# Silu on ScalarE in place of the tanh form, and the first layer's sums moved from VectorE to ScalarE

## The chip, the cores and the metric

The kernel runs on one core of one Trainium2 chip. Its metric is the device time of one execution in microseconds. The engines are named as in the profile: PE is TensorE (PEld its weight loads), DVE is VectorE, ACT is ScalarE, POOL is GpSimd, SP is SyncE, which issues nearly all of the DMAs. Every engine works through its own list of instructions in order; semaphores hold an instruction back until what it reads is there.

## What is computed

The input is x, 16 batches of 512 tokens with 256 features, all float32. Four layers follow one another, each on the normalized x and added to x:

```python
x = x + mamba(layernorm(x), ...)        # selective scan: h = exp(dt*A)*h + inp, 16 states per feature
x = x + ffn(layernorm(x), ...)          # the same FFN weights twice
x = x + linear_attention(layernorm(x), ...)   # 16 heads of 16, causal
x = x + ffn(layernorm(x), ...)
```

The FFN quantizes its input, its weights and its hidden values to 4-bit floats in blocks of 16 along the last dimension, and computes

```python
gate = fp4_linear(x, w_gate)            # 256 -> 704
y    = fp4_linear(x, w_up)              # 256 -> 704
h    = silu(gate) * y                   # silu(g) = g * sigmoid(g) = 0.5 * g * (1 + tanh(g/2))
return fp4_linear(h, w_down)            # 704 -> 256
```

## The kernel before

A batch goes through four stages: `scan` (mamba and, woven into it, the prologue of the next batch), the first FFN (`ffn` with the letter "f"), `attention`, and the second FFN (`last_ffn`, letter "g"). Each stage is a Python generator; what it yields is the cost in microseconds of VectorE that it puts on its last piece. `run_all` (L866) keeps several stages under way and always draws from the one that is least far on, its progress being the yielded cost over the constant of its kind (`SCAN, FFN, ATTN`, L863). So at one time the scan of batch b, the first FFN of batch b-1, the attention of batch b-2 and the second FFN of batch b-3 are written into the engines' lists piece by piece. The constants and the yields thus decide how the stages lie among one another. After the weights' preparation and the first scans the program repeats itself from batch to batch; below, one such repeat is called a period.

In `scan`, each batch takes 16 steps (L533 to L575). A step needs a tile `bar` of two rows of 512: it is fetched by a DMA from DRAM (L520), ACT raises it to exponentials (Exp at L527, twice, then Square at L530), DVE scans over it (L548) and multiplies (L552), and PE sums it over the states (L558). There are four `bar` buffers, so a fetch is issued when the scan of four steps earlier has ended, and ACT has it next in its list after the other work that was written ahead of it.

`front` (L435) is the first part of the prologue. It takes the mean and variance of the coming batch's x for the first layer's normalization: `bn_stats` (L442) and `bn_aggr` (L443) on DVE for each of the four chunks of 128 tokens, then `inverse` (L389), a small DVE instruction and a power on POOL that give 1/sqrt(var + eps). `to_features` (L412) turns x into features by rows with diagonal matrices that ACT makes of the result (L424). For the other layers the sums come from elsewhere: DVE adds up the row sums while it adds the residual (`residual`, L373), and ACT adds up the squared distances from the mean (`distances`, L382 to L386, an activation Square with bias and an accumulated sum).

`ffn` (L583) normalizes, quantizes (`fp4_steps`, L225), transposes, and then goes over four chunks of 128 tokens. `hidden` (L596) computes one chunk's 704 hidden values in two halves of 352. Per half, PE fills two PSUM banks, `pg` with the gate and `pu` with the up projection (L605, two matmuls each over the contraction); ACT computes tanh(gate/2) (L611); DVE computes (1 + tanh) * gate (L612) and then 0.5 * that * up (L613). Then `fp4` quantizes the hidden chunk: five DVE passes over 704 elements, with one on ACT between them (L248, the tile `big`). `down` (L619) transposes it on PE, ACT copies it out of PSUM (L631, L636, tile `hqT`), and PE multiplies by the down weights (L640); DVE adds the result to x (L377 or L647). There are seven PSUM banks for all that passes through `bank`.

ACT's functions come in table sets, and an instruction that loads a table stands in its list wherever the next function is in another set than the last. Before, ACT uses Exp, Tanh, Ln, Abs, Relu, Square and copies. Its list holds 33 table loads: 16 ahead of the Ln at L472, 16 ahead of the next Tanh (L611) or Exp (L527) that follows it, and one at the start.

Of the kernel before, what the change touches and what calls it, by code (L numbers as in the profile page):

```python
# [32 lines left out]
def kernel(  # L33
# [45 lines left out]
    def bank(name):  # L79
        return ps.tile([P, 512], F32, tag="bank", name=name)  # L80
# [287 lines left out]
    def summed(i, name):  # L368

        sums = small.tile([P, NC], F32, tag=f"sum{i}", name=f"sum_{name}")  # L370
        dist = small.tile([P, NC], F32, tag=f"dist{i}", name=f"dist_{name}")
        return sums, dist
# [16 lines left out]
    def inverse(i, var, by, name):  # L389

        shifted = small.tile([P, NC], F32, tag=f"var{i}", name=f"var_{name}")
        nc.vector.tensor_scalar(shifted, var, by, LN_EPS, ALU.mult, ALU.add)
        rstd = small.tile([P, NC], F32, tag=f"rstd{i}", name=f"rstd_{name}")
        nc.gpsimd.tensor_tensor(rstd, shifted, neg_half, ALU.pow)
        return rstd
# [38 lines left out]

    def front(b, xt):  # L435

        stats = small.tile(
            [P, NC, nc.vector.BN_STATS_DIM], F32, tag="stats", name=f"st_m{b}"
        )
        mv = small.tile([P, NC, nc.vector.BN_AGGR_DIM], F32, tag="mv", name=f"mv_m{b}")  # L440
        for c in range(NC):
            nc.vector.bn_stats(stats[:, c, :], xt[:, c, :])  # L442
            nc.vector.bn_aggr(mv[:, c, :], stats[:, c, :])  # L443
        rstd = inverse(2, mv[:, :, 1], 1.0, f"m{b}")
        yield 2.4
        turned[b] = to_features(one, xt, f"m{b}", rstd)
        yield 1

# [134 lines left out]
    def ffn(i, nm, b, xs):  # L583
        xt = xs[b]
        act = acts[i]
        xq = layernorm(i, xt, stats.pop((nm, b)), f"{nm}{b}")
        if i == 0:
            stats["a", b] = summed(2, f"a{b}")
        key, nm = ("a", b), f"{nm}{b}"
        yield 2.2  # L590
        fp4(act, xq.rearrange("p c d -> p (c d)"), NC * D, nm)
        yield 7
        xqT = to_features(act, xq, nm)
        yield 1

        def hidden(c):  # L596

            h = act.tile([P, FF], F32, tag="h", name=f"h_{nm}_{c}", bufs=2)
            for f in range(2):
                cols = ts(f, HF)  # L600
                pg = bank(f"pg_{nm}_{c}_{f}")
                pu = bank(f"pu_{nm}_{c}_{f}")
                for pw, wT in ((pg, wgT), (pu, wuT)):
                    for k in range(ND):
                        nc.tensor.matmul(  # L605
                            pw[:, :HF], xqT[:, k, ts(c, P)], wT[:, k, cols],
                            start=(k == 0), stop=(k == ND - 1),
                        )

                hc = h[:, cols]  # L610
                nc.scalar.activation(hc, pg[:, :HF], AF.Tanh, scale=0.5)  # L611
                nc.vector.scalar_tensor_tensor(hc, hc, 1.0, pg[:, :HF], ALU.add, ALU.mult)  # L612
                nc.vector.scalar_tensor_tensor(hc, hc, 0.5, pu[:, :HF], ALU.mult, ALU.mult)  # L613
                yield 1
            fp4(act, h, FF, f"{nm}_{c}")
            hs.append(h)
            yield 5

        def down(c, h):  # L619

            hqT = act.tile([P, NR, P], F32, tag="hqT", name=f"hqT_{nm}_{c}", bufs=2)
            for r0 in range(0, NR, 4):
                r1 = min(r0 + 4, NR)
                pt = bank(f"pt_h_{nm}_{c}_{r0}")
                for r in range(r0, r1):
                    rows = min(P, FF - r * P)
                    nc.tensor.transpose(
                        pt[:rows, ts(r - r0, P)], h[:, r * P : r * P + rows], ident
                    )
                full = min(r1, NF)  # L630
                nc.scalar.copy(  # L631
                    hqT[:, r0:full, :],
                    pt[:, : (full - r0) * P].rearrange("p (r t) -> p r t", t=P),
                )
                if r1 > NF:
                    nc.scalar.copy(hqT[:TAIL, NF, :], pt[:TAIL, ts(NF - r0, P)])  # L636
            po = bank(f"po_{nm}_{c}")
            for r in range(NR):
                rows = min(P, FF - r * P)
                nc.tensor.matmul(  # L640
                    po[:, :D], hqT[:rows, r, :], wdT[:rows, r, :],
                    start=(r == 0), stop=(r == NR - 1),
                )
            if key in stats:
                residual(xt, c, po[:, :D], stats[key])
            else:
                nc.vector.tensor_tensor(xt[:, c, :], xt[:, c, :], po[:, :D], ALU.add)  # L647


        hs = []  # L650
        yield from hidden(0)
        for c in range(NC):
            if c + 1 < NC:
                yield from hidden(c + 1)
            down(c, hs[c])
            yield 0.5
# [203 lines left out]
        nc.sync.dma_start(out[b].rearrange("(c p) d -> p c d", p=P), xs[b])  # L860


    SCAN, FFN, ATTN = 65.7, 40.2, 25.7  # L863

    def run_all(stages):

# [62 lines left out]
```

## Time and profile before

| | |
|---|---|
| median of 3 runs | 2825.38 us (2824.58 to 2828.75) |
| the profiled execution's own time | 2823.49 us |
| its span, first to last instruction | 2821.8 us |
| mean granted TensorE clock | 0.942 |
| period, from one Ln load (L472) to the next | 162 to 165 us |
| first Ln load of a fully mixed period, last Ln load | 595.7 us, 2245.8 us |
| ACT busy in one period (911 to 1074 us) | 92.06 of 163 us |

The span thus has a fill of nearly 600 us, ten like periods, and a drain of nearly 580 us in which no scan is left. Busy time of an engine is the time in which one of its instructions was on record; consecutive instructions of DVE and ACT overlap by some 0.1 us in the records. "Idle before" is the time an engine stood still ahead of an instruction, with who ended it.

### The profile page before, as it was taken

What the parts mean: (1) busy time and instruction counts of PE and PEld (TensorE: products, weight loads), DVE (VectorE), ACT (ScalarE), POOL (GpSimd) and SP (SyncE); (2) the same over time, 40 slices, a digit from 0 to 9 for tenths busy, and PEclk for the clock granted to TensorE, in tenths of its full rate; (3) what the DMA queues carried; (4) which work ended last, traced back from release to release, by engine and by line L of the source; (5) the groups of instructions that cost most, each with busy time, mean ns of one, the idle gap of its engine ahead of it and who ended that gap; (6) DMA issues with size and microseconds to landing.
All of it is one profiled execution on the core that took longest, in us unless ns stands there. A gap on an engine that the chain in (4) does not pass through costs nothing.

```text
span 2821.8 us, 34272 instructions
## 1 busy us (share of the span) xinstructions
PE 2449.7 (87%) x12907; PEld 1441.9 (51%) x12907; DVE 2430.5 (86%) x3689; ACT 1492.1 (53%) x2846; POOL 172.2 (6%) x171
## 2 busy tenths in 40 slices
PE   5677989799898989989898998989899898889886
PEld 3234545455555555555555555555555554556564
DVE  7898888898999898899989889998988999868465
ACT  4776564465646455464645556464555646333321
POOL 2000000000000010000001000000100000000000
PEclk7788999899999999999999999999999999999897
DMA  5533212222223131322313132131213213000000
GB/s 142 131 93 82 64 49 53 67 53 83 52 60 76 38 75 45 82 53 54 82 38 75 45 82 53 47 89 38 75 45 83 53 45 82 24 8 1 8 8 8
DMA packets 97146, 165.01 MB, mean 58 GB/s; under 512 B 8434, under 2 KB 92372, under 8 KB 96980
## 3 DMA queue, kind: packets, MB, share of 16 engines
q1 hardware_dynamic: 95360, 161.77, 22.3%
q8 instruction: 101, 1.65, 0.3%
q10 hardware_dynamic: 1620, 1.06, 0.1%
q14 instruction: 65, 0.53, 0.1%
HBM read 146.02 MB, written 16.78 MB: 58 GB/s over the span
## 4 chain that ended last, share of the span: by engine, by line
DVE 40%; PE 36%; DMA 9%; ACT 9%; issue 3%; POOL 2%; SPq 0%; POOLq 0%; ACTq 0%; DVEq 0%
DVE h L548 15%; DMA bar<-dd 9%; PE pg_g L605 5%; DVE h L552 4%; PE pu_g L605 4%; PE po_g L640 4%; PE pg_f L605 3%; PE pu_f L605 3%; PE py L558 3%; ACT bar L527 2%; PE pz L457 2%; DVE v_f L244 2%; DVE sm L729 2%; PE pqk L678 2%; ACT bar L530 1%
## 5 line engine op out<-in xcount | busy, mean ns | idle before, releaser
L548 DVE TENSOR_TENSOR_SCAN h<-bar,inp 128x1024 f32<-128x1024 f32 x256 | 579.4, 2277 | 13.9 <-PE py L558 7.6
L527 ACT ACTIVATE bar<-bar,a_col 128x511 f32<-128x511 f32 x512 | 352.4, 715 | 339.6 <-DMA bar<-dd 291.5
L558 PE MATMUL py<-h,red 128*32 128x512 f32 x1024 | 288.7, 645 | 119.3 <-DVE h L552 118.2
L552 DVE TENSOR_TENSOR h<-h,cm 128x1024 f32<-128x1024 f32 x256 | 311.1, 1218 | 0.6
L530 ACT ACTIVATE bar<-bar 128x1022 f32<-128x1022 f32 x256 | 269.3, 1052 | 3.0
L640 PE MATMUL po_g<-wdT,hqT_g 128*128 128x256 f32 (+1 forms) x768 | 214.3, 425 | 41.8 <-ACT hqT_g L631 41.8
L640 PEld LDWEIGHTS po_g<-wdT,hqT_g 128*128 128x128 f32 (+1 forms) x768 | 149.0, 206 | 120.3 <-ACT hqT_g L631 65.1
L640 PE MATMUL po_f<-wdT,hqT_f 128*128 128x256 f32 (+1 forms) x768 | 198.2, 400 | 9.6 <-ACT hqT_f L631 9.6
L605 PE MATMUL pg_g<-wgT,tT_g 128*128 128x352 f32 x512 | 190.7, 492 | 0.3 <-DVE sm L729 0.3
L640 PEld LDWEIGHTS po_f<-wdT,hqT_f 128*128 128x128 f32 (+1 forms) x768 | 137.5, 192 | 94.6 <-ACT hqT_f L636 29.0
L605 PE MATMUL pu_g<-wuT,tT_g 128*128 128x352 f32 x512 | 182.3, 480 | 0.0
L605 PE MATMUL pg_f<-wgT,tT_f 128*128 128x352 f32 x512 | 181.8, 478 | 0.0
L605 PE MATMUL pu_f<-wuT,tT_f 128*128 128x352 f32 x512 | 172.7, 460 | 3.4 <-DVE sm L729 3.0
L729 DVE TENSOR_TENSOR sm<-psc,causal 128x512 f32<-128x512 f32 x256 | 163.9, 681 | 10.8 <-PE psc L722 5.9
L611 ACT ACTIVATE h_g<-pg_g 128x352 f32<-128x352 f32 x128 | 59.1, 462 | 195.3 <-PE pg_g L605 195.1
L558 PEld LDWEIGHTS py<-h,red 128*32 128x32 f32 x1024 | 37.8, 110 | 221.6 <-DVE h L552 171.4
L605 PEld LDWEIGHTS pu_g<-wuT,tT_g 128*128 128x128 f32 x512 | 103.3, 202 | 60.7 <-issue 11.4
L763 POOL COPY dx<-den 128x256 f32<-128x256 f32 x64 | 42.2, 660 | 1482.7 <-PE pr L768 795.5
L248 ACT ACTIVATE big_f<-v_f 128x704 bf16<-128x704 f32 (+1 forms) x80 | 67.2, 840 | 122.3 <-DVE v_f L244 122.3
L605 PEld LDWEIGHTS pg_f<-wgT,tT_f 128*128 128x128 f32 x512 | 96.3, 196 | 66.9 <-issue 23.2
L612 DVE SCALAR_TENSOR_TENSOR h_g<-h_g,pg_g 128x352 f32<-128x352 f32 x128 | 65.5, 512 | 74.2 <-ACT h_g L611 72.8
L678 PE MATMUL pqk<-tT_a,w_qkv_sb 128*128 128x512 f32 x256 | 121.6, 614 | 7.4 <-ACT tT_a L430 7.4
(237 smaller groups left out, 4707.0 us busy)
## 6 DMA issues: line engine op xcount, KB each, us to landing
bar<-dd SPq DMA_DIRECT2D x256, 511.0 KB, 4.7
x<-in_L_attn_a_x_dram SPq DMA_DIRECT2D x16, 512.0 KB, 4.5
dd<-dt SPq DMA_DIRECT2D x128, 64.0 KB, 1.7
out_dram<-x SPq DMA_DIRECT2D x16, 512.0 KB, 4.4
w_qkv_sb<-in_L_attn_b_W_attn_dram ACTq DMA_DIRECT2D x1, 768.0 KB, 7.1
raw_d<-in_L_ffn_w_down_dram SPq DMA_DIRECT2D x1, 704.0 KB
raw_g<-in_L_ffn_w_gate_dram SPq DMA_DIRECT2D x1, 640.0 KB, 7.1
raw_u<-in_L_ffn_w_up_dram SPq DMA_DIRECT2D x1, 640.0 KB, 6.5
```

The source lines that it names most:

```text
L248: nc.scalar.activation(big, v, AF.Abs, scale=STEP)
L527: nc.scalar.activation(bar[:, i, 1:S], bar[:, i, 1:S], AF.Exp, scale=a_col[:, g : g + 1])
L530: nc.scalar.activation(bar[:, :, 1:S], bar[:, :, 1:S], AF.Square)
L548: nc.vector.tensor_tensor_scan(h.rearrange("p i t -> p (i t)"), bar.rearrange("p i t -> p (i t)"), inp.rearrange("p i t -> p (i t)"), 0.0, ...
L552: nc.vector.tensor_tensor(h, h, cm.unsqueeze(1).to_broadcast([P, 2, S]), ALU.mult)
L558: nc.tensor.matmul(py[32 * q : 32 * q + 32, :], red[:, j, :], (h0, h)[q // 2][:, q % 2, :], start=False, stop=(j == 3),)
L605: nc.tensor.matmul(pw[:, :HF], xqT[:, k, ts(c, P)], wT[:, k, cols], start=(k == 0), stop=(k == ND - 1),)
L611: nc.scalar.activation(hc, pg[:, :HF], AF.Tanh, scale=0.5)
L612: nc.vector.scalar_tensor_tensor(hc, hc, 1.0, pg[:, :HF], ALU.add, ALU.mult)
L640: nc.tensor.matmul(po[:, :D], hqT[:rows, r, :], wdT[:rows, r, :], start=(r == 0), stop=(r == NR - 1),)
L678: nc.tensor.matmul(pz, w_qkv_sb[:, k, ts(je, P)], xnT[:, k, :], start=(k == 0), stop=(k == ND - 1),)
L729: nc.vector.tensor_tensor(t, psc[g].rearrange("p (s t) -> p s t", t=P), causal.unsqueeze(1).to_broadcast([P, NH // 4, P]), ALU.mult,)
```

## The change

It has three parts. In `hidden`, the gate banks of both halves are filled one behind the other, ACT computes Silu of each directly into h, and after a yield the two up banks are filled and DVE multiplies them in with one instruction per half; the DVE instruction with the gate (L612) is gone. In `front`, ACT takes the place of DVE: a Copy with an accumulated sum for each chunk, then the squared distances by the helper that the other layers use. And the constants and yields by which the stages are interleaved are lowered.

```diff
     def front(b, xt):
 
-        stats = small.tile(
-            [P, NC, nc.vector.BN_STATS_DIM], F32, tag="stats", name=f"st_m{b}"
-        )
-        mv = small.tile([P, NC, nc.vector.BN_AGGR_DIM], F32, tag="mv", name=f"mv_m{b}")
+        sums, dist = summed(0, f"m{b}")
         for c in range(NC):
-            nc.vector.bn_stats(stats[:, c, :], xt[:, c, :])
-            nc.vector.bn_aggr(mv[:, c, :], stats[:, c, :])
-        rstd = inverse(2, mv[:, :, 1], 1.0, f"m{b}")
-        yield 2.4
+            nc.scalar.activation(squares, xt[:, c, :], AF.Copy, accum_out=sums[:, c : c + 1])
+            distances(xt, c, sums, dist)
+        rstd = inverse(2, dist, 1.0 / D**3, f"m{b}")
+        yield 0.2
         turned[b] = to_features(one, xt, f"m{b}", rstd)
         yield 1
...
             h = act.tile([P, FF], F32, tag="h", name=f"h_{nm}_{c}", bufs=2)
-            for f in range(2):
-                cols = ts(f, HF)
-                pg = bank(f"pg_{nm}_{c}_{f}")
-                pu = bank(f"pu_{nm}_{c}_{f}")
-                for pw, wT in ((pg, wgT), (pu, wuT)):
+
+            for wT, what in ((wgT, "pg"), (wuT, "pu")):
+                for f in range(2):
+                    cols = ts(f, HF)
+                    pw = bank(f"{what}_{nm}_{c}_{f}")
                     for k in range(ND):
                         nc.tensor.matmul(
                             pw[:, :HF], xqT[:, k, ts(c, P)], wT[:, k, cols],
                             start=(k == 0), stop=(k == ND - 1),
                         )
-
-                hc = h[:, cols]
-                nc.scalar.activation(hc, pg[:, :HF], AF.Tanh, scale=0.5)
-                nc.vector.scalar_tensor_tensor(hc, hc, 1.0, pg[:, :HF], ALU.add, ALU.mult)
-                nc.vector.scalar_tensor_tensor(hc, hc, 0.5, pu[:, :HF], ALU.mult, ALU.mult)
-                yield 1
+                    if what == "pg":
+                        nc.scalar.activation(h[:, cols], pw[:, :HF], AF.Silu)
+                    else:
+                        nc.vector.tensor_tensor(h[:, cols], h[:, cols], pw[:, :HF], ALU.mult)
+                yield 0.5
             fp4(act, h, FF, f"{nm}_{c}")
...
-    SCAN, FFN, ATTN = 65.7, 40.2, 25.7
+    SCAN, FFN, ATTN = 63.5, 36.2, 25.7
```

In the lists of instructions that the changed program gives the engines, there are 192 table loads on ACT where there were 33: one at the start, 16 ahead of the Ln, 87 ahead of a Silu, 88 ahead of an Exp (86 of the scan's, 2 of the attention's). The numbers of PE's, POOL's and SP's instructions are the same but for the merging of rows, and their order is another where the stages are interleaved otherwise.

## The prediction

> **What bounds the kernel now.** I read the page's busy shares first: DVE and PE are both near nine tenths, ACT at half.
>
> ```profile
> PE 2449.7 (87%) x12907; PEld 1441.9 (51%) x12907; DVE 2430.5 (86%) x3689; ACT 1492.1 (53%) x2846; POOL 172.2 (6%) x171
> ...
> DVE 40%; PE 36%; DMA 9%; ACT 9%; issue 3%; POOL 2%; SPq 0%; POOLq 0%; ACTq 0%; DVEq 0%
> ```
>
> The chain that ended last passes to and fro between DVE and PE, with ACT on it for 9% of the span (about 260 us, a sixth of ACT's busy time). Then the busy times by windows, for one period:
>
> ```profile
> 911.00:950.00 39.00, 37.74 (x157) 23.70 (x158) 33.42 (x62) 22.46 (x36) 0.84 (x1) 0.96 0.15 37
> ...
> 911.00:1074.00 163.00, 147.90 (x802) 87.12 (x802) 147.92 (x227) 92.06 (x176) 10.27 (x9) 0.98 0.24 61
> ```
>
> After the length, the columns are PE, PEld, DVE and ACT busy. PE and DVE carry 148 us each of 163, so neither alone sets the period: their imbalance stretch by stretch does. In the first 39 us, the gate and up products of the FFNs, PE is full and DVE waits. Next the groups by line and the waits:
>
> ```profile
> L612 DVE SCALAR_TENSOR_TENSOR h_f<-h_f,pg_f 128x352 f32<-128x352 f32 x128 | 65.8, 515 | 68.2 <-ACT h_f L611 68.1
> L612 DVE SCALAR_TENSOR_TENSOR h_g<-h_g,pg_g 128x352 f32<-128x352 f32 x128 | 65.5, 512 | 74.2 <-ACT h_g L611 72.8
> ...
> L442 DVE BATCH_NORM_STATS2 st_m<-x 128x6 f32<-128x256 f32 x64 | 24.3, 398 | 0.1
> ```
>
> ```profile
> ACT bar L527 <- DMA bar<-dd: 291.5, 152, 6.1
> ACT h_g L611 <- PE pg_g L605: 195.1, 96, 5.8
> ```
>
> L612, which the change removes, is also where DVE waits longest (141 us). But the second fence shows where that comes from: ACT itself waits there for PE's gate product, and elsewhere it stands at the head of its list for a `bar` fetch (291 us), with all behind it held.
>
> **DVE's saving.** Records of DVE overlap: an L612 of 0.51 us at 917.79 is followed by L819 at 918.22. With overlaps counted once, the 256 L612 hold 119 us and the `bn_stats` and `bn_aggr` rows (64 each) 26 us. L613 becomes a product of the same two operands and keeps its 507 ns (L647 with 256 elements takes 414 and L729 with 512 takes 681, which puts 352 at 514, so between no change and 2 us in all). DVE falls by 145 us, from 2430 to 2285, 9 us a period.
>
> **What of it counts.** PE's work is unchanged. To see what DVE's saving is worth I cut a period at the last up product of each of its eight chunks, where DVE needs PE (L613, in its place the new product), and added up for each engine the durations of the instructions that its list has between two cuts. Before, DVE/PE in us: up to g0 54.0/52.7, f0 4.4/2.5, g1 8.1/7.0, f1 6.0/6.8, g2 6.8/12.7, g3 23.7/20.2, f2 12.5/16.3, f3 34.3/33.7. The larger of each pair add up to 160.3; measured, the ten periods from 700.2 to 2350.0 took 165.0 each, so 4.7 are other waits. The changed program, by its own lists and the same durations, DVE/PE/ACT: 53.4/51.8/46.4, 4.1/5.0/0.8, 5.5/7.0/1.6, 7.5/7.5/8.4, 9.5/11.5/8.4, 12.1/20.7/10.5, 17.1/15.7/8.6, 31.6/32.7/26.9. The largest of each add up to 155.8. So of DVE's 9 us about half is lost: the products with the gate stood where PE is the later one, and the lowered constants move three scan steps out from under PE's chunks g2 and g3. Worth 4.4 us a period, 44 us in ten. In the drain after 2350 the same sum falls from 401 to 383 us, by 18; it is PE that sets most of it, and the other order packs it better. In the fill up to 700 us it falls by 10.
>
> **ACT's new work.** A table load is a row of its own; here one pair in ACT's timeline:
>
> ```profile
> 924.07 0.46 ACT L611 ACTIVATE h_g<-pg_g 128x352 f32<-128x352 f32 x1
> 924.55 1.28 ACT L472 ACT_TABLE_LOAD   x1
> 925.84 1.15 ACT L472 ACTIVATE soft<-soft,half_c 128x1024 f32<-128x1024 f32 x1
> 927.01 1.28 ACT L611 ACT_TABLE_LOAD   x1
> ```
>
> From the end of the activation ahead (924.53) to the start of the next one 1.31 us pass, and the usual overlap of 0.1 is lost: 1.40 us each. With 192 loads for 33 that is 159 x 1.40 = 223 us. The Trainium skill speaks against this change: "ScalarE: Activation LUTs", in its rules for kernel authors, has activations grouped by table set, and its section on what a load costs gives about 2.66 us a switch, a drain of 1.38 us included. By the rule it would be 423 us, ACT 73% busy. The row shows no such gap: the next activation starts 0.01 us after the load. I take 1.40. Silu on the same tile is taken at Tanh's 460 ns (a cheap or dear function on other tiles here differs by tens of ns: on 128x512, 691 for Exp and 690 for Relu), so zero to +-5 us in all. For the sums, 64 Square with accumulator (506 + 189 ns) at L384 are the near row for the 64 distances; the Copy lies between a plain copy of 256 (369) and that, plus the read: 0.6 to 0.7 us. Together 64 x 1.3 = 84 us, 5.2 a period. ACT comes to about 1800 us, 64%.
>
> **What hides it.** A load carries no wait, so ACT does it ahead of waiting for the function's operand. (At 43.52 before, a load for Exp was followed by 6.06 us of waiting for `bar`.) A Silu's load lies in the wait for the gate product (96 waits of 2.0 us for g alone), and Silu itself is done while PE fills the up banks for 2.4 us, so DVE's wait at L612 is gone there. An Exp's load lies in the wait for `bar` (152 of 1.9 us). The sums fall where ACT waited 0.5 to 1.8 us between two diagonals (L424) because PE still read the last one. Where ACT has no such wait the loads come through, with what is queued behind: `big` (DVE waits for it at L250, 50 us in all before), `hqT` (PE at L640, 51), `num` and `kt` (L760, L779), and the Exp of the step after next. In a period I count these places: at f2 the two Silu stand apart, with an Exp that waits for `bar` and two loads between them, but DVE has two scans and two products (about 9.5 us) ahead of needing them, against some 7 us on ACT; at f3 a load comes behind three fetched `bar` (+1.4), but the wait of 3.5 us that DVE had at L612 there (1027 us) is shortened since ACT has less queued before it (-3); then `num` and `kt` are behind a load and an Exp that waits for its fetch (+2); the sums at the scan-dense stretch, where ACT rises from 41.1 to 46.4 of 53.4 (+1.5); loads among g1, f1 and g2, where ACT is as full as PE (+1.5). Sum about +3 a period, +30 in ten. The mixed periods of the fill have the same loads and ACT is the fullest engine in some of their stretches: +10, which uses up what the sum gives there. The drain has hardly any Exp left, and so few loads: nothing.
>
> **Sum.** -44 + 30 - 10 + 10 - 18 = -32 us on the profiled span of 2821.8, so 2790; its time was 1.7 more and the median of the runs another 1.9: 2793, rounded to 2795.
>
> **The rivals.** (1) ACT's work comes through: slower. The chain has a sixth of ACT's time on it. If the added 307 us come through at that rate, +51 against the -72 of the cuts would still be a gain; but ACT's idle share falls from 47% to 36%, and the waits behind it in an in-order list grow faster than its load. If 40% come through (two of five loads find no wait to hide in), +123 - 72 = +51: 2876. If 30%, +92 - 72: 2845, the middle of this rival. It decides from about 23%, and its place is the stretch from f2 to g0, where Silu and Exp alternate and `num`, `kt` and `big` queue behind them. For it: 291 us of ACT's waiting are fetches with work held behind. Against it: loads need no operand. (2) The gain is used up exactly: DVE only waits longer for PE, which has 148 us in every period, and the cuts' 4 us go to ACT: 2825, within 0.2%, which is about what a measurement of this kernel can tell from no change. (3) More is gained: PE runs ahead over the cuts (before, g2 took 7.7 us where the sum says 12.7), ACT hides all loads, and the drain loses a part of its other waits too: -72 - 15 = 2738 or somewhat above.
>
> **How the numbers follow.** The forecast (2762 to 2819) 0.44; (3), below 2762, 0.07; (2) 0.09; (1) 0.40, of which 0.10 above 2880. The range from 2758 to 2880 leaves about 0.16 out, and takes in both ends of the unknown costs. Faster by over 0.2%: 0.51; within: 0.09; slower: 0.40. The forecast's own range is 2762 to 2819.
>
> **What would show it.** Right: DVE busy about 2285, PE unchanged near 2450, ACT near 1800 with 192 loads of 1.28 us; periods of 162 to 164 us where the cuts now have 165; DVE's waits for ACT at the product with up below 60 us in all; the drain shorter by some 18 us. Wrong: DVE's waits for `big`, `num` and the new product, or PE's for `hqT` and `kt`, grown together by more than DVE's saving; rows that show a gap of over 1 us around a load; or periods of 167 us and more, with `bar` ready too late for L548 (4.9 us of waits before).

## The result, and the profile after

The changed kernel takes 2854.24 us (median of 4 runs, 2842.42 to 2855.51), the kernel before beside it 2826.86 us (2824.58 to 2828.75): a ratio of 1.0088 with a 95% interval of 1.006 to 1.0116. It is slower by 25 us by the ratio and 27 by the medians, and 59 us above the forecast. The profiled execution took 2853.58 us with a span of 2851.9 us; its mean granted clock was 0.925, where it was 0.942 before.

First the page's busy shares and the shares of the chain that ended last:

```profile
PE 2441.2 (86%) x12907; PEld 1463.7 (51%) x12907; DVE 2313.1 (81%) x3305; ACT 1745.8 (61%) x3261; POOL 178.5 (6%) x171
...
DVE 37%; PE 37%; ACT 17%; POOL 3%; DMA 3%; issue 3%; SPq 0%; POOLq 0%; ACTq 0%; DVEq 0%
```

The busy times are much as forecast: DVE 2313 (2285), PE unchanged, ACT 1746 (1800). But ACT's share of the chain has grown from 9% to 17%, that of the fetches has fallen from 9% to 3%. In the groups by line (busy us, mean ns, then idle time ahead and what ended it) one sees who took the place of L612:

```profile
L524 ACT ACTIVATE bar<-bar,a_col 128x511 f32<-128x511 f32 x512 | 349.1, 714 | 152.9 <-DMA bar<-dd 107.2 <-DVE x L643 30.6 <-DVE x L377 6.9
L607 ACT ACT_TABLE_LOAD x87 | 111.6, 1283 | 1.5
L524 ACT ACT_TABLE_LOAD x86 | 110.3, 1283 | 8.8 <-DMA bar<-dd 7.3
...
L609 DVE TENSOR_TENSOR h_g<-h_g,pu_g 128x352 f32<-128x352 f32 x128 | 65.1, 516 | 52.9 <-PE pu_g L602 51.3 <-ACT big_g L248 0.8 <-ACT h_g L607 0.5
L609 DVE TENSOR_TENSOR h_f<-h_f,pu_f 128x352 f32<-128x352 f32 x128 | 63.5, 514 | 65.5 <-ACT h_f L607 38.7 <-PE pu_f L602 26.5
```

DVE's 141 us of waiting for ACT at L612 have become 39 us of waiting for ACT and 78 for PE at L609. ACT waits 107 us for `bar` where it waited 291; in the changed program's own lists without the loads (the fifth group below) it waits 214, so the loads fill 107 us of that wait, as the prediction had it. Among PE's own waits there is an exchange:

```profile
PE pt_a L426 <- ACT diag_a L424: 87.7, 16, 5.8
PE po_g L636 <- ACT hqT_g L627: 63.0, 39, 4.8
...
PE py L555 <- DVE h L549: 47.8, 20, 6.7
```

Before, these three stood at 24.4, 41.8 and 118.2 us: PE waits less for DVE, and more for ACT's diagonals and `hqT`. The exchange is not the loads' doing: in the same lists without them the three are 87.7, 61.2 and 45.5.

Cut at the last up product of f3 of the fourth and of the fourteenth batch, as in the prediction, the span falls into a fill, ten periods and a drain:

| us | fill | ten periods | drain | span |
|---|---|---|---|---|
| before | 700.2 | 1649.8 | 471.8 | 2821.8 |
| after | 718.0 | 1668.5 | 465.4 | 2851.9 |
| difference | +17.8 | +18.7 | -6.4 | +30.1 |
| predicted | 0 | -14 | -18 | -32 |

### The profile page after: what moved, and what is told of

Its sections match the earlier page's. It is cut to its first block, busy times and chain, and to the rows that moved or that the text cites. A ratio compares the mean times of both kernels' runs of the same rounds, so it can differ in the third digit from the quotient of the medians.

```text
span 2851.9 us, 34191 instructions
## 1 busy us (share of the span) xinstructions
PE 2441.2 (86%) x12907; PEld 1463.7 (51%) x12907; DVE 2313.1 (81%) x3305; ACT 1745.8 (61%) x3261; POOL 178.5 (6%) x171
## 3 DMA queue, kind: packets, MB, share of 16 engines
q8 instruction: 101, 1.65, 0.2%
## 4 chain that ended last, share of the span: by engine, by line
DVE 37%; PE 37%; ACT 17%; POOL 3%; DMA 3%; issue 3%; SPq 0%; POOLq 0%; ACTq 0%; DVEq 0%
DVE h L545 13%; PE po_g L636 6%; DVE h L549 5%; PE pg_g L602 4%; PE pu_g L602 3%; ACT bar L524 3%; PE pg_f L602 3%; PE pu_f L602 3%; DMA bar<-dd 3%; PE py L555 2%; PE po_f L636 2%; ACT bar L527 2%; PE pro L796 2%; PE pn L749 2%; ACT big_f L248 1%
## 5 line engine op out<-in xcount | busy, mean ns | idle before, releaser
L545 DVE TENSOR_TENSOR_SCAN h<-bar,inp 128x1024 f32<-128x1024 f32 x256 | 578.8, 2279 | 44.7 <-PE py L555 32.7
L555 PE MATMUL py<-h,red 128*32 128x512 f32 x1024 | 253.3, 657 | 48.1 <-DVE h L549 47.8
L636 PE MATMUL po_g<-wdT,hqT_g 128*128 128x256 f32 (+1 forms) x768 | 230.0, 449 | 63.0 <-ACT hqT_g L627 63.0
L636 PE MATMUL po_f<-wdT,hqT_f 128*128 128x256 f32 (+1 forms) x768 | 197.9, 400 | 21.6 <-ACT hqT_f L627 21.6
L636 PEld LDWEIGHTS po_f<-wdT,hqT_f 128*128 128x128 f32 (+1 forms) x768 | 136.9, 191 | 100.1 <-ACT hqT_f L627 39.3
L602 PE MATMUL pu_f<-wuT,tT_f 128*128 128x352 f32 x512 | 166.8, 465 | 11.7 <-DVE sm L725 11.6
L602 PE MATMUL pg_g<-wgT,tT_g 128*128 128x352 f32 x512 | 172.3, 480 | 3.3 <-DVE sm L725 2.4
L602 PE MATMUL pu_g<-wuT,tT_g 128*128 128x352 f32 x512 | 163.2, 462 | 9.1 <-DVE sm L725 9.1
L602 PE MATMUL pg_f<-wgT,tT_f 128*128 128x352 f32 x512 | 169.1, 473 | 0.8 <-ACT tT_f L419 0.6
L248 ACT ACTIVATE big_g<-v_g 128x704 bf16<-128x704 f32 (+1 forms) x80 | 67.3, 842 | 116.9 <-DVE v_g L244 116.9
L426 PE MATMUL pt_a<-diag_a,x 128*128 128x128 f32 x256 | 61.0, 432 | 87.7 <-ACT diag_a L424 87.7
L602 PEld LDWEIGHTS pu_f<-wuT,tT_f 128*128 128x128 f32 x512 | 95.0, 190 | 72.3 <-DVE sm L725 18.4
L602 PEld LDWEIGHTS pu_g<-wuT,tT_g 128*128 128x128 f32 x512 | 95.1, 190 | 64.3 <-DVE sm L725 15.8
L602 PEld LDWEIGHTS pg_g<-wgT,tT_g 128*128 128x128 f32 x512 | 94.9, 195 | 58.2 <-issue 14.0
```

The lines of the kernel that those rows point to most:

```text
L248: nc.scalar.activation(big, v, AF.Abs, scale=STEP)
L426: nc.tensor.matmul(pts[k][:, ts(c, P)], t[:, c, ts(k, P)], diag, start=True, stop=True)
L545: nc.vector.tensor_tensor_scan(h.rearrange("p i t -> p (i t)"), bar.rearrange("p i t -> p (i t)"), inp.rearrange("p i t -> p (i t)"), 0.0, ...
L555: nc.tensor.matmul(py[32 * q : 32 * q + 32, :], red[:, j, :], (h0, h)[q // 2][:, q % 2, :], start=False, stop=(j == 3),)
L602: nc.tensor.matmul(pw[:, :HF], xqT[:, k, ts(c, P)], wT[:, k, cols], start=(k == 0), stop=(k == ND - 1),)
L636: nc.tensor.matmul(po[:, :D], hqT[:rows, r, :], wdT[:rows, r, :], start=(r == 0), stop=(r == NR - 1),)
```

## The experiments

Two questions: what do the table loads cost (the theory: they come through where ACT has no wait left to hide them), and what is DVE's saving worth (the prediction's theory: half of it; the rival: nearly nothing, since PE or a chain of waits is late anyway). A third came up on the way: every edit lets the builder write the engines' lists in another order. So in the first four groups a difference between two kernels holds the edit and the new order together. Each kernel is compared with runs of the kernel before on the same chip, which had medians of 2829.5, 2827.5, 2821.2, 2828.0 and 2827.2 us in the five groups below; where kernels of different groups are set against each other, the difference by the ratios to these is given too if it is another.

### First group: the change taken apart

**no_loads**: the change with Tanh for Silu.

```diff
-    nc.scalar.activation(h[:, cols], pw[:, :HF], AF.Silu)
+    nc.scalar.activation(h[:, cols], pw[:, :HF], AF.Tanh)
```

> Tanh stands where Silu did, with the same number of instructions; the hidden value is tanh(gate) * up, not the reference's. Tanh is in Exp's table set, so 33 loads in place of 192. Loads theory (the 159 loads are what was added to the waits): periods fall from 166.9 to some 160 to 162 us and the fill by 10 to 20, in all 2740 to 2775. Order theory (the three scan steps that moved out from under PE's chunks are the loss): little change, 2835 to 2850. Sums theory (ACT's sums hold back the diagonals for PE): PE's wait for the diagonals of the attention stays near 88 us, and 2820 to 2845.

Measured: 2816.01 us (2813.24 to 2818.08), ratio 0.9953 [0.9938, 0.9968]. Without loads the change is a small gain; the time lies between the expectations. By this pair the 159 loads cost 38 us, but ACT's and PE's lists are not quite the same in the two.

**old_order**: the change with the yields and constants of before.

```diff
-        yield 0.2
+        yield 2.4
...
-                yield 0.5
+                yield 1
...
-    SCAN, FFN, ATTN = 63.5, 36.2, 25.7
+    SCAN, FFN, ATTN = 65.7, 40.2, 25.7
```

> The changed kernel with the yields and constants of before (2.4 for the front, 1 per pair of banks, 65.7 and 40.2); 169 loads. Order theory: the scan steps go back under PE's chunks, 2800 to 2820. Loads theory: 10% fewer loads, otherwise as the changed kernel, 2840 to 2860. Sums theory: 2845 to 2860.

Measured: 2843.78 us (2840.81 to 2850.45), 1.0055 [1.0037, 1.0073]. At the old pace the change is 10 us faster by the medians, and still slower than the kernel before, as the loads theory had it: the lowered constants are not the cause as a whole.

**silu_only**: the change with `bn_stats` and `bn_aggr` back in `front` (yield 2.4, SCAN 65.7, FFN 36.2).

> Silu with both gates one behind the other, but bn_stats on DVE as before (constants 65.7 and 36.2); 178 loads. Sums theory: PE's wait for the attention's diagonals falls back from 88 to about 25 us and the time to 2800 to 2825. Loads theory: ACT has 84 us less but most loads, 2835 to 2850. Order theory: 2835 to 2855.

Measured: 2884.58 us (2882.13 to 2891.89), 1.0201 [1.018, 1.0223]: far slower than the whole change and than any expectation.

**sums_only**: the kernel before with the change's `front` alone (yield 0.2, SCAN 63.5, FFN 40.2).

> The kernel before with only the first layer's sums moved to ACT (constants 63.5 and 40.2); 33 loads, ACT 84 us busier, DVE 26 us less. Sums theory: slower, 2845 to 2865, with PE waiting some 60 us more for diagonals. Loads theory: 2815 to 2830, since ACT's idle time takes the sums. Order theory: 2825 to 2840.

Measured: 2822.96 us (2819.22 to 2829.38), 0.9977 [0.9967, 0.9987]. The sums on ACT are a small gain; that points to the FFN part for the loss.

### Second group: DVE, PE, grouping and loads on the kernel before

**no_gate_op**: the kernel before without L612.

```diff
                 nc.scalar.activation(hc, pg[:, :HF], AF.Tanh, scale=0.5)
-                nc.vector.scalar_tensor_tensor(hc, hc, 1.0, pg[:, :HF], ALU.add, ALU.mult)
```

> The kernel before without L612, the DVE instruction with the gate: the hidden value is 0.5 * tanh(gate/2) * up. Order of the gates, constants and sums as before, 33 loads. PE theory (the chunks' stretch is PE's, and the scan-dense stretch waits on chains through ACT and the fetches, so DVE's time there is not on the path): 2805 to 2832. DVE theory (the saving is real and the new order lost it): 2760 to 2795.

Measured: 2819.46 us (2812.55 to 2827.87, 20 runs), 0.9971 [0.9961, 0.9981]. DVE is busy 108 us less (its L612 held 119 with overlaps counted once), the time is 8 us less. DVE now waits 224 us for PE instead of 96. The granted clock is lower too, 0.928 for 0.942, so this is not the price of the instruction alone.

**half_up**: the kernel before with one of the up product's two contraction steps left out.

```diff
-                    for k in range(ND):
+                    ks = range(1 if pw is pu else ND)
+                    for k in ks:
...
-                            start=(k == 0), stop=(k == ND - 1),
+                            start=(k == 0), stop=(k == ks[-1]),
```

> The kernel before with one of the two contraction steps of the up product left out (only 128 of 256 features count), which takes some 88 us of PE's time and nothing from DVE or ACT. PE theory: the stretch of six chunks falls from 66 to about 62 us, where DVE takes over, and the period by 3 to 5: 2770 to 2795. DVE theory: under 10 us, 2818 to 2830.

Measured: 2740.21 us (2734.56 to 2742.48), 0.9683 [0.9661, 0.9705], lower than either expectation. Its busy line:

```profile
PE 2301.5 (84%) x12395; PEld 1348.8 (49%) x12395; DVE 2421.0 (88%) x3689; ACT 1498.3 (55%) x2846; POOL 195.3 (7%) x171
```

148 us less for PE (88 had been expected) gave 87 us: 0.6 of PE's time came through, 0.07 of DVE's in no_gate_op. In both the lists moved as well.

**gates_first**: the kernel before with both gate banks of a chunk filled ahead of both up banks; Tanh and both DVE products stay, a yield of 1 after each pair.

```diff
-                for pw, wT in ((pg, wgT), (pu, wuT)):
+            for wT, what in ((wgT, "pg"), (wuT, "pu")):
+                for f in range(2):
...
+                    if what == "pg":
+                        nc.scalar.activation(hc, pw[:, :HF], AF.Tanh, scale=0.5)
+                        nc.vector.scalar_tensor_tensor(hc, hc, 1.0, pw[:, :HF], ALU.add, ALU.mult)
+                    else:
+                        nc.vector.scalar_tensor_tensor(hc, hc, 0.5, pw[:, :HF], ALU.mult, ALU.mult)
                 yield 1
```

> The kernel before with both gate banks filled ahead of both up banks, Tanh and both DVE instructions kept, constants as before, 33 loads. If the regrouping itself costs (PE waits for banks that DVE still reads): 2840 to 2860. If it does not: 2818 to 2835.

Measured: 2805.77 us (2799.44 to 2810.58), 0.9916 [0.9892, 0.9941]. The regrouping that the change brings along is a gain by itself in the order that the builder then writes, more than either expectation.

**loads_added**: gates_first with Silu for Tanh, both DVE products kept.

```diff
-                        nc.scalar.activation(hc, pw[:, :HF], AF.Tanh, scale=0.5)
+                        nc.scalar.activation(hc, pw[:, :HF], AF.Silu, scale=0.5)
```

> The same with Silu of gate/2 in Tanh's place, so that only table loads are added: 235 for 33 (the hidden value is not the reference's). Loads theory, with the rate of 38 us for 159 loads that the changed kernel showed against its copy with Tanh: 45 to 60 us above the kernel with the gates first. If ACT's idle time hides them: under 15 us above it.

Measured: 2863.28 us (2861.14 to 2875.6), 1.013 [1.0101, 1.0159]: 57 us for 202 loads, 0.28 each. The order moved too: PE's wait for `diag_a` went from 23 to 93 us.

### Third group: what combines, and two more pairs for the loads

**gates_sums**: gates_first with the change's `front` (yield 0.2, SCAN 63.5, FFN 40.2).

> Both gate banks ahead of both up banks with Tanh and both DVE instructions, and the first layer's sums on ACT (constants 63.5 and 40.2); 33 loads, nothing left out. The parts alone gave -22 and -6.5 us. If they add: 2792 to 2805, faster than both kernels. If ACT's sums collide with the new order: 2808 to 2825.

Measured: 2774.24 us (2772.76 to 2782.59), 0.9841 [0.9821, 0.9862]. It is the change without Silu and without the lowered FFN pace, it beats both kernels, and it is below both expectations.

**no_loads_old**: old_order with Tanh for Silu.

> The changed kernel with Tanh for Silu (hidden value tanh(gate) * up) and the yields and constants of before; 33 loads. If the lowered constants are what keeps the copy without loads (2816) above the kernel with the gates first (2806): 2785 to 2800. If the DVE instruction that is gone is simply worth nothing once PE sets the chunks' stretch: 2800 to 2820.

Measured: 2849.95 us (2843.09 to 2853.26), 1.0097 [1.0075, 1.0118], no faster than old_order with its 169 loads (2843.78; 12 us slower by the ratios). It is above both expectations: either the loads cost nothing in that order, or the order moved against them.

**silu_no_loads**: silu_only with Tanh for Silu.

> Silu part alone, bn_stats kept on DVE, with Tanh for Silu (hidden value tanh(gate) * up), 33 loads. The same with Silu took 2884 with 178 loads. At the rate of 0.24 to 0.28 us a load the 145 loads are worth 35 to 41 us: 2840 to 2850. If the loads alone make that kernel so slow (its wait for the attention's diagonals is 120 us): 2805 to 2825.

Measured: 2841.29 us (2836.25 to 2842.8), 1.0063 [1.0041, 1.0086], 43 us below silu_only (39 by the ratios) for 145 loads, as the rate of the earlier pairs had it.

**more_dve**: the kernel before with one DVE product more per half.

```diff
                 nc.vector.scalar_tensor_tensor(hc, hc, 1.0, pg[:, :HF], ALU.add, ALU.mult)
+                nc.vector.tensor_tensor(hc, hc, pg[:, :HF], ALU.mult)
```

> The kernel before with one more DVE instruction per half, a product with the gate bank after L612 (the hidden value has the gate twice), some 119 us more of DVE. PE theory: DVE overtakes PE in the stretch of chunks by a few us a period and the rest waits anyway: 2840 to 2880, well under half of what is added. DVE theory: 2910 to 2950.

Measured: 2873.35 us (2868.01 to 2881.98), 1.0186 [1.0162, 1.021]. DVE busy rose by 108 us to 2539, the time by 52, as the PE theory had it. One more DVE instruction seemed to cost six times what one less brought, which made the order the suspect: here too PE's wait for `diag_a` is 89 us.

### Fourth group: instruction or pace

In the copy without loads (2816) DVE is busy 95 us less than in gates_sums (2774), and it is slower. The first two kernels below change one thing of gates_sums each; the third puts Silu into the first of them.

**gs_no_op**: without the DVE product with the gate.

```diff
-                        nc.vector.scalar_tensor_tensor(hc, hc, 1.0, pw[:, :HF], ALU.add, ALU.mult)
```

> The regrouped kernel with ACT's sums (2774 us) without the DVE instruction that multiplies by 1 + tanh; the constants stay. It leaves out that factor of the gate, so only its time is read. DVE has about 119 us less to do. If the instruction is as little worth here as in the kernel before (-8 us), 2763 to 2774. If DVE's saving is what the constants of the change spoiled, up to 44 us come: 2730 to 2755. If taking the instruction away itself brings the loss of the copy without loads (PE's next chunk is pulled ahead of work that others wait for), 2790 to 2816.

Measured: 2806.25 us (2802.9 to 2810.95), 0.9916 [0.9896, 0.9935]. Less work, 32 us more time (21 by the ratios), as the third expectation had it.

**gs_pace**: with the change's FFN pace.

```diff
-                yield 1
+                yield 0.5
...
-    SCAN, FFN, ATTN = 63.5, 40.2, 25.7
+    SCAN, FFN, ATTN = 63.5, 36.2, 25.7
```

> The regrouped kernel with ACT's sums (2774 us), with the change's FFN pace: 0.5 at each of the two yields and 36.2 for 40.2. DVE keeps its instruction and ACT its 33 loads. If the lowered pace is what makes the copy without loads slow, 2800 to 2825. If the pace costs nothing, 2766 to 2782, and the missing instruction is the suspect.

Measured: 2845.18 us (2840.51 to 2850.99), 1.0051 [1.0034, 1.0069]. The same instructions in another order: 71 us (59 by the ratios), above both expectations.

**gs_silu**: with Silu and the single product, at the FFN's old pace.

> The change at the FFN's old pace (yields of 1, 40.2): Silu, one product on DVE, sums on ACT, 211 table loads where the regrouped kernel with the sums has 33. It computes the reference. If loads cost 0.24 to 0.30 us each as in three pairs so far, 43 to 53 us above the kernel without the DVE instruction: 2810 to 2830 if that one is near 2770. If the loads of the old order cost nothing, as in one pair, the same as it within 8 us. The prediction's sum, with DVE's saving at 44 and the loads at 30, would give 2760.

Measured: 2838.11 us (2835.88 to 2856.36, 13 runs), 1.0047 [1.003, 1.0064]; 32 us above gs_no_op for 178 loads, 0.18 each, where 43 to 53 had been expected. Neither pace makes the Silu form a gain.

The two effects don't add up: the pace costs 59 to 71 us with the DVE instruction and some 10 us without it (2806 for gs_no_op, 2816 for no_loads, which differ in the pace and in the form of the remaining product). So single prices could not be had from kernels whose lists move.

### Fifth group: lists held fixed

Here the lists are built as always, and only then one instruction's function or width is replaced, with its waits and signals kept. Order and semaphores are instruction by instruction those of the kernel named; what alone changes besides is where table loads stand.

```diff
     with _tile.TileContext(nc) as tc:
         tile_mamba_fp4ffn_linattn_fp4ffn_kernel(tc, *args)
+    swap(nc)
...
+            if isinstance(i, mybir.InstActivation) and i.func == AF.Silu and "h_" in str(i.outs[0]):
+                i = mybir.InstActivation(
+                    name=i.name, func=AF.Tanh, ins=i.ins, outs=i.outs, engine=i.engine,
+                    sync_info=i.sync_info, debug=i.debug,
+                )
```

These lines are those of the first kernel; for the other two kernels the DVE products that read `pg` are rebuilt with 8 columns in the same manner.

**after_same_list_no_loads**:

> The changed program with its lists exactly as they are, but with Tanh as the function of the 256 gate activations (DVE's factor is missing, so only the time is read): 159 table loads fall away and nothing moves. If the copy without loads of the first call (2816) told their price, 2810 to 2822. If a part of those 38 us was the order, 2825 to 2845. If the loads cost the 30 to 40 us that the prediction took, 2814 to 2824; if they are all hidden, 2848 to 2856.

Measured: 2805.07 us (2804.26 to 2805.53), 0.9919 [0.9901, 0.9937], below every expectation: 49 us for 159 loads, 0.31 each, 22% of the 1.40 taken. ACT is busy 1542.5 us for 1745.8, so 1.28 us per load.

**before_same_list_narrow**:

> The program before with its lists exactly as they are, but with the DVE product with the gate done on 8 of its 352 columns (the rest of that factor is left out, so only the time is read): about 90 us of DVE's work fall away and nothing moves. If DVE is the bound in the stretches in which it has more work, as the prediction's cuts have it, half of it comes: 2780 to 2790. If PE sets those stretches too, -5 to -20: 2808 to 2823. If all of DVE's time counts, 2738.

Measured: 2801.33 us (2800.77 to 2809.34), 0.9916 [0.989, 0.9942]: -24 us by the ratio, between two expectations. The spans tell where. The fill went from 700.2 to 688.1 us, the drain from 471.8 to 462.4, the ten periods from 1649.8 to 1648.6. In the ten periods 160 of these instructions lost 0.36 us each, 57 us, and 1.2 us came of it. The clock has no part in that: in both programs' ten periods its records show it at one half for 92 us. DVE's waits for ACT take it up; the narrow kernel's own list of them:

```profile
DVE h_g L612 <- ACT h_g L611: 87.7, 55, 5.5
DVE h_f L612 <- ACT h_f L611: 75.5, 40, 5.3
DVE v_g L250 <- ACT big_g L248: 59.7, 50, 4.1
...
DVE v_f L250 <- ACT big_f L248: 15.9, 22, 2.6
```

Before, these four were 72.8, 68.1, 42.0 and 7.7: 48 us more waiting, for 92 us less work.

**gs_same_list_narrow**:

> The regrouped kernel with ACT's sums (2774 us), its lists exactly as they are, with the DVE product with the gate done on 8 of 352 columns. Without that instruction at all the builder wrote other lists, and it took 2806. If the order was the cause of the 32 us, this one is at or below 2774: 2750 to 2774. If DVE's shorter work itself does it (PE's and ACT's work then meet at worse times), 2790 to 2810.

Measured: 2766.28 us (2760.77 to 2769.51), 0.978 [0.9759, 0.9802], 8 us below gates_sums by the medians and 17 by the ratios, as the order theory had it. gs_no_op has no more work than this kernel and takes 2806: some 40 us are the order of the lists alone.

## Why the prediction was wrong

With the lists held fixed, the loads and the rest of the change can be told apart in each part of the span. Before to after_same_list_no_loads is all but the loads; from there to after is the loads. The cuts at g0, f2 and f3 part each of the ten periods into three stretches: from f3 to g0, the six chunks up to f2, and from f2 to f3. The predicted columns put the prediction's sums and terms into the stretches that they were meant for; the 15 are for the first layer's sums on ACT, which belong to the rest.

| us | rest, predicted | rest, measured | loads, predicted | loads, measured |
|---|---|---|---|---|
| fill | -10 | +3.2 | +10 | +14.6 |
| f3 to g0, ten times | -6 + 15 | +7.3 | +20 | +27.8 |
| six chunks, ten times | -23 | -18.3 | +15 | +2.3 |
| f2 to f3, ten times | -16 | -2.6 | -16 | +2.3 |
| drain | -18 | -8.0 | 0 | +1.6 |
| sum | -57 | -18.4 | +25 | +48.5 |

(By single terms the predicted columns add up to -58 and +29; the prediction rounded within a period.) The sums are -32 as predicted and +30.1 as measured; of the 62 us between them 38.6 are the rest and 23.5 the loads.

**The step that failed** is "What of it counts": the larger sum of two engines between two cuts, with "the same durations" of their instructions, was taken as the time of the stretch, and the fall of these sums, 72 us in all, as what the change brings. The windows of one period show it, cut in the three stretches and, for two of the programs, as a whole. The columns are length, PE, PEld, DVE, ACT and POOL busy, the granted clock, the DMA share and GB/s. Before:

```profile
1360.30:1420.70 60.40, 51.98 (x259) 30.19 (x259) 55.59 (x87) 41.75 (x81) 4.83 (x3) 0.94 0.21 53
1420.70:1486.70 66.00, 61.37 (x318) 36.97 (x316) 59.30 (x97) 28.73 (x55) 1.24 (x2) 1.00 0.16 41
1486.70:1524.80 38.10, 34.60 (x235) 19.99 (x228) 34.15 (x47) 21.62 (x41) 4.20 (x4) 1.00 0.45 111
1360.30:1524.80 164.50, 147.94 (x803) 87.15 (x802) 149.04 (x230) 92.10 (x176) 10.27 (x9) 0.98 0.24 61
```

The changed program's lists without the loads:

```profile
1356.00:1417.10 61.10, 50.42 (x272) 29.45 (x264) 55.52 (x84) 43.19 (x95) 7.48 (x5) 0.94 0.11 26
1417.10:1481.40 64.30, 62.61 (x332) 39.20 (x330) 54.74 (x87) 29.46 (x58) 2.45 (x3) 1.00 0.26 64
1481.40:1520.70 39.30, 34.03 (x199) 20.02 (x198) 31.78 (x35) 22.43 (x41) 1.45 (x1) 0.87 0.45 111
1356.00:1520.70 164.70, 147.06 (x799) 88.67 (x790) 142.03 (x205) 95.08 (x192) 11.38 (x9) 0.95 0.25 61
```

And after:

```profile
1384.90:1448.60 63.70, 51.20 (x256) 29.33 (x256) 55.62 (x84) 44.19 (x96) 7.48 (x5) 0.92 0.09 25
1448.60:1513.10 64.50, 62.59 (x329) 39.35 (x328) 54.73 (x87) 39.49 (x65) 2.45 (x3) 1.00 0.27 63
1513.10:1549.50 36.40, 31.76 (x223) 18.97 (x222) 31.94 (x36) 25.66 (x44) 0.42 (x2) 1.00 0.48 121
```

In the six chunks PE is busy 62.6 of 64.3 us: it sets them, and they give 1.8 us on the mean of ten periods (66.1 to 64.3) where the sums had said 2.3 (72.0 to 69.7). DVE's shorter work there (59.3 to 54.7) is not what gives it: in before_same_list_narrow DVE has 3.3 us a period less in these chunks, nothing else is changed, and they take 66.7. What is left is the other order.

In the other two stretches no engine is full. The level of the sums shows it: measured before are 60.9, 66.1 and 37.9 us for sums of 54.0, 72.0 and 34.3. So the 4.7 us of "other waits" that the prediction knew of, and let stay as they were, are +6.9, -5.9 and +3.6. In the seven and four us that lie over the sums the engines wait for one another, and these waits did not stay as they were.

The term that the prediction put at nothing is PE's clock. The clock records of the traces show it at one or at one half, in steps of 3.4 us:

| us at half clock | fill | f3 to g0, ten times | six chunks, ten times | f2 to f3, ten times | drain |
|---|---|---|---|---|---|
| before | 153.6 | 85.3 | 3.4 | 3.4 | 83.7 |
| before_same_list_narrow | 139.9 | 85.3 | 6.8 | 0 | 70.0 |
| after_same_list_no_loads | 157.0 | 75.1 | 0 | 61.4 | 93.7 |
| after | 177.5 | 122.9 | 0 | 37.5 | 90.2 |

In the ten periods of before, after_same_list_no_loads and after, the clock fell to one half 69 times, and each time PE had been busy for half or less of the 3.4 us just before; of the 1266 other pieces of 3.4 us at full clock, only 12 had it busy for less than half. So a wait of PE that is long enough is paid twice here, and from f2 to f3 one sees it. First before, then the changed lists without loads:

```profile
1490.55 3.05 PE L640 MATMUL po_g<-wdT,hqT_g 128*128 128x256 f32 x12 [1.91 <-ACT hqT_g L631]
```

```profile
1485.28 5.78 PE L636 MATMUL po_g<-wdT,hqT_g 128*128 128x256 f32 x12 [2.84 <-ACT hqT_g L627]
```

In the new order PE has two `py` matmuls ahead of this wait where it had eight, waits longer, and then does the same twelve matmuls at half clock. The 1.6 us a period that the sums give this stretch (34.3 to 32.7) do come where the clock stays up: 36.4 to 36.7 us in the three periods without loads that have only 3.4 us at half clock, 36.4 to 36.9 in the five of after that have none, for 37.9 on the mean before. In the other seven without loads it took 37.5 to 39.3. No run holds the clock fixed, so how the missing 13 us divide between the clock and the waits is not shown.

In the fill and the drain the sum failed by 13 and 10 us. The fixed list of before shows that DVE's time does come through there (22 us of the 23 by which its span fell, with 14 us less at half clock in each), so what the change lost again must lie in the other order or in ACT's sums; which of the two was not tried with fixed lists.

**DVE's saving** was itself a little large: its busy time fell by 117 us for 145. Alone, the gate's product took 108 off (no_gate_op) and the sums 18 (sums_only), where the prediction had 119 and 26.

**ACT's new work** was sized well: 192 loads of 1283 ns, no gap; the sums' rows at L439 and L384 add up to 82 us for 84; busy 1746 us for 1800. The rule of the Trainium skill in "ScalarE: Activation LUTs" that speaks against the change had the right sign of its effect; its 2.66 us a switch would have made ACT 71% busy by the prediction's own terms (1492 + 423 + 84 of 2822 us; its 73% is a slip), measured are 61%.

**What hides it** failed in two terms, the credit at f3 and, again, the clock. Two places in ACT's timeline after, at f2 and at the end of f3:

```profile
1506.23 0.44 ACT L607 ACTIVATE h_f<-pg_f 128x352 f32<-128x352 f32 x1
1506.69 1.28 ACT L524 ACT_TABLE_LOAD   x1
1509.00 0.72 ACT L524 ACTIVATE bar<-bar,a_col 128x511 f32<-128x511 f32 x1 [1.03 <-DMA bar<-dd]
1509.74 1.28 ACT L607 ACT_TABLE_LOAD   x1
1511.04 0.46 ACT L607 ACTIVATE h_f<-pg_f 128x352 f32<-128x352 f32 x1
...
1545.69 1.05 ACT L527 ACTIVATE bar<-bar 128x1022 f32<-128x1022 f32 x1
1546.77 1.28 ACT L607 ACT_TABLE_LOAD   x1
1548.06 0.82 ACT L607 ACTIVATE h_f<-pg_f 128x352 f32<-128x352 f32 x2
1548.90 1.28 ACT L524 ACT_TABLE_LOAD   x1
```

and the latter place in the same list without loads:

```profile
1518.35 1.05 ACT L527 ACTIVATE bar<-bar 128x1022 f32<-128x1022 f32 x1
1519.31 0.80 ACT L607 ACTIVATE h_f<-pg_f 128x352 f32<-128x352 f32 x2
```

The load at 1506.69 is hidden: the fetch still ends 1.03 us after it. The one at 1546.77 is not: no instruction around it has idle time ahead, Silu is done 1.3 us later, and another load stands ahead of what follows. As both lists are the same, each DVE instruction can be paired with its twin, and one can see where the lag grows. In the ten periods it grows by 12.2 us at h_f times up (L609), by 20.2 at `yT` (L769, which waits for `num`), by 11.2 at `v` (L250, which waits for `big`) and by 6.2 at x (L377, which waits for PE's `pro`), and falls by 13.2 and 6.3 where DVE was early anyway (L643, h_g at L609). The prediction had +1.4 and +2 a period for the first two (measured 1.2 and 2.0), but took 3 us off at f3 because ACT "has less queued before it". That credit did not come, and of the 1.5 put down for g1, f1 and g2 only 0.2 did. The fill was undersized by 5.

Of the loads' 32.3 us in the ten periods 27.8 lie between f3 and g0, and there again the clock has a part. Behind f3 of the period above, after and without loads:

```profile
1388.62 0.71 PE L780 MATMUL pkv<-vpad,kt 128*128 128x128 f32 x4 [2.75 <-ACT kt L775]
1389.27 1.76 PE L555 MATMUL py<-h,red 128*32 128x512 f32 x2
1390.96 2.06 PE L796 MATMUL pro<-w_o_sb,yT 128*128 128x256 f32 x4
```

```profile
1358.71 0.71 PE L780 MATMUL pkv<-vpad,kt 128*128 128x128 f32 x4 [0.93 <-ACT kt L775]
1359.36 1.04 PE L555 MATMUL py<-h,red 128*32 128x512 f32 x2
1360.33 1.13 PE L796 MATMUL pro<-w_o_sb,yT 128*128 128x256 f32 x4
```

A load ahead of an Exp (1384.32) puts `num` and `kt` back, PE waits 2.75 us for `kt` instead of 0.93 (1.0 of the 1.8 more is the later `kt`, 0.8 that PE is there sooner), and the clock is at one half from 1389.5 to 1392.9: `py` and `pro` take 1.65 us more, of 2.6 by which DVE then lags. In nine of the ten periods after, the clock falls within 5 us of f3, without the loads in none. In the one period without this fall the stretch takes 0.8 us longer than its twin without loads (61.1), in the worst 6.5 us longer than its own (61.7):

```profile
718.00:779.90 61.90, 49.42 (x257) 28.85 (x256) 55.41 (x84) 44.97 (x97) 7.48 (x5) 0.94 0.11 26
1881.60:1949.80 68.20, 55.52 (x254) 31.57 (x253) 55.62 (x84) 44.42 (x96) 7.23 (x5) 0.85 0.09 24
```

Whole periods with the same time at half clock differ by less than the mean of 3.2 us: with 10.2 us at half clock 162.0 without loads and 164.4 to 164.6 with them, with 13.7 us 162.6 to 164.8 and 165.4, with 17.1 us 164.7 and 166.7 to 167.7. An estimate from these: some 2 us a period would remain at an equal clock, and 1 goes with the lower one. The four runs of after agree with that: the fastest, 2842.42 us, has the highest mean clock, 0.929, the other three 0.924 to 0.925.

**The rivals.** The one that ended slower came, at 2854 for its 2845, but by a smaller price than it had: the loads came through at 22%, and by its own arithmetic "about 23%" would only have used up a gain of 72 us. The gain was 18.4, ACT's sums already taken off, and the end of the stretch that this rival named, f3 to g0, is where most of the loads' price lies. The even case and the larger gain did not come.

**What would show it.** Right: ACT's and PE's busy times, the loads' 1.28 us, DVE's waits for ACT at the product (39 us, below 60). Wrong: periods of 166.9 for 162 to 164, the drain 6 us shorter for 18. The sign given for a failure, waits for `num`, `kt` and `hqT` grown together, came in part: DVE's wait for `num` 11.6 to 30.7, PE's for `kt` 21.6 to 48.1, for `hqT_g` 41.8 to 63.0. Without the loads these are 12.7, 28.8 and 61.2: the first two are for the most part the loads', the third is the order's.

**Still open.** Why the list of gates_sums, with the product narrowed, is 40 us better than that of gs_no_op, and why the change's pace costs 59 to 71 us there and 10 elsewhere, is shown in size only. The clock goes along with both: its mean is 0.945 in gs_same_list_narrow and 0.931 in gs_no_op, 0.939 in gates_sums and 0.930 in gs_pace. Which waits of PE the order lengthens was not followed up there. PE's wait for `diag_a`, about 20 us in some lists and about 90 in others, does not settle it: where it is long, PE's wait for the scan's h is short (after, 88 and 48; before, 24 and 118). More buffers for `bar` were not tried.

## What to carry to other kernels

Ahead of counting an engine's saving, set the length of each stretch against every engine's sum in it. Here a shorter DVE brought next to nothing in the ten periods (57 us gave 1.2), where PE fills one stretch and chains of waits set the two others. Read the granted clock of the stretch beside the sums: a sum of durations holds only as long as the clock does, and here it fell where a new order or a load let PE stand idle for half of 3.4 us or more. Table loads hid in an in-order engine's waits, but not behind work that was already late: 0.31 us of 1.28 came through with 100 us of waiting for fetches still left, and that was more than the whole rest of the change brought. Where a builder orders the lists, price an edit with the lists held fixed before believing any difference below what a new order makes (here up to some 60 or 70 us); of the runs here the tanh form with both gates first and the sums on ACT was the fastest that computes the reference, 2774 us.

## What the runs showed of the hardware

- A table load took 1283 ns whatever function it was for, and an activation that had nothing to wait for started 0.01 to 0.02 us after it. Silu took 460 to 463 ns on 128x352, Tanh in the same places 455 to 462.
- DVE's product took 512 to 515 ns on 352 columns and 153 to 157 on 8: 1.04 ns a column and about 147 ns fixed. A narrow instruction is far from free.
- Matmuls took longer at half clock: four `pro` 2.06 us for 1.13, twelve `po_g` 5.78 for 3.05. With the same lists PE was busy 2416.5 us without the loads, at a mean granted clock of 0.931, and 2441.2 with them, at 0.925.
- With the same lists PE's wait for `diag_a` was 87.7 us in 16 places both with the loads and without them; its wait for `kt` went from 28.8 to 48.1.
